# Three vector operations moved to GpSimd and two units moved to the front of an image's first attention block

## The chip, the cores and the metric

The kernel runs on one core of one Trainium2 chip. The metric is the device time of one execution in microseconds (us). Before the change it is 7322.82 us, the median of three runs (7321.42 to 7324.19).

## What is computed

Four images of 128 channels and 64 x 64 pixels go through two layers. In the first, every image is group-normalised and goes through an attention over its 4096 pixels whose keys, queries and values come from 1 x 1 convolutions. In the second, the pixels are tokens of 128 numbers. Each token is normalised, and 16 heads of 8 numbers attend over the tokens; query, key and value of a head are one and the same vector, made from cosines:

```
c = cos(heads + rx_theta);  P = cumprod(c);  z0 = prod(c[1:])
q = [z0, P[1:]]                                  # 16 heads of 8
scores = q q^T / sqrt(8);  ctx = softmax(scores) q
x1 = layernorm(x + ctx w_comb^T + b);  t = t + feed_forward(x1)
```

A recurrence over the tokens, y = sigmoid(W x + V y), ends the work. The change touches the cosine of one chunk of tokens and the order of the first work of the second layer's attention.

## The kernel before, in words

Images are worked on one after the other. For each there is a convolution stage (first_stage: the first layer, with the feed-forward of the image before woven in) and an attention stage (second_stage, which calls attention). The 4096 tokens are eight chunks of 512. For a chunk, the generator `tokens` (L465) takes the first layer's result, normalises it (statistics L249 and L250, a reciprocal root on GpSimd at L228, the normalisation L255), adds rx_theta (L518, the argument of the cosine), brings the argument into range with `cos_steps` (L233 and L234 give k, the number of turns; L235, L237 and L238 subtract k times two pi in three parts; L240 takes the magnitude), lets ScalarE take the sine (L242), multiplies the cosines up (L536 to L541), turns the result with TensorE (L273, tile pq) and writes it to DRAM as high and low parts (L557). Seven chunks are done within the convolution stage. The last one, called the tail here, is carried into the attention stage, where one step of it is taken in each turn of the attention's first block: statistics after the third unit, the normalisation and argument two turns later, then the steps of the cosine, the sine in the tenth step, the products after it.

The attention works on two heads at a time, a pair; there are eight pairs. A pair has four blocks of 1024 queries. A block is a list of units, each a pair of tiles of 128 keys, and one turn of the loop works on one unit. Since scores are symmetric, only about half of them are computed. A unit of the block's own keys (an own unit) is used once. An off unit is used twice: for its own queries, and mirrored for the queries of the other block. In a turn:

- TensorE computes the scores of a unit (L867) into two of three score tiles in PSUM, the accumulators. ScalarE exponentiates them (L879); for off units it also sums them, and some off units are split in two halves, with an instruction for each.
- TensorE weighs the values with the exponentials of the unit two turns earlier (L720).
- For an off unit, VectorE transposes its two exponential tiles (L686, in `run_flips`). Four off units make a group. Two turns after a group's fourth transposition its sixteen mirrored steps (L699, `mirror_step`) may begin; each turn does as many as a credit allows, about three. When a group's sixteen steps are done, VectorE adds the product to a running sum (L713). The transposed tiles of two groups are held at once, and so are two mirrored products. Transposes of group g wait until the steps of group g - 2 are done.

An exponential tile comes free when its weighing and its transposition are done; there are six such tiles, three units' worth, and part of the image's input tile is used as further room in some turns.

All this is written in a manual schedule: each of TensorE, ScalarE, VectorE and GpSimd works through its own queue in exactly the order in which the program states its instructions. A wait in front of one instruction holds everything behind it on that engine. In VectorE's queue, the tail's steps thus stand between the transposes.

The function `order` gives the sequence of the units in a block. In the blocks of the first half, with 16 off and 4 own units, it is four off units and an own one, four times over. `prepare` loads keys and queries for a pair, in the order in which the units ask for them. After the last pair a drain works off what is left of transposes and mirrored steps, interleaved with the next image's statistics (L307 to L321), and GpSimd gathers the sums (L747, L787, L789).

Of the kernel before, what the change touches and what calls it, by code (L numbers as in the profile page):

```python
# [13 lines left out]
ALU = mybir.AluOpType  # L14
# [8 lines left out]
ROUND = 1.5 * 2**23  # L23
# [3 lines left out]
def kernel(  # L27
# [31 lines left out]
    nc = tc.nc  # L59
# [168 lines left out]
        nc.gpsimd.tensor_tensor(r, v, minus_half[: shape[0], : shape[1]], ALU.pow)  # L228
        return r

    def cos_steps(dst, arg, k, r):

        nc.vector.tensor_scalar(k, arg, 1.0 / (2 * math.pi), ROUND, ALU.mult, ALU.add)  # L233
        nc.vector.tensor_scalar(k, k, ROUND, None, ALU.subtract)  # L234
        nc.vector.scalar_tensor_tensor(r, k, -TWO_PI_1, arg, ALU.mult, ALU.add)  # L235
        yield
        nc.vector.scalar_tensor_tensor(r, k, -TWO_PI_2, r, ALU.mult, ALU.add)  # L237
        nc.vector.scalar_tensor_tensor(r, k, -TWO_PI_3, r, ALU.mult, ALU.add)  # L238
        yield
        nc.vector.scalar_tensor_tensor(r, r, -1.0, r, ALU.mult, ALU.max)  # L240
        yield
        nc.scalar.activation(dst, r, AF.Sin, bias=half_pi[: dst.shape[0]], scale=-1.0)  # L242
# [222 lines left out]
    def tokens(im, i, sums):  # L465

        n, q, cols = im["n"], im["q"], ts(i, IC)
        last = i == NTG - 1  # L470
        yield

        pt = transposed(blocks(im["xs"][:, cols]), f"px{n}_{i}", "ps_tok")
        x0 = im["xs"][:, cols] if last else get("thalf", f"x0_{n}_{i}")
        nc.scalar.copy(x0, pt)
        yield


        total, taken = sums.pop(i), sums.pop(("sum", i))
        ps = get("ps_tok", f"sum{n}_{i}")[:, 0:P]  # L480
        tv = total.rearrange("p j (k c r) -> p j c k r", c=4, r=32)
        for j in range(2):
            for c in range(4):
                nc.tensor.matmul(
                    ps[ts(c, 32), :],
                    ones[:, 0:32],
                    tv[:, j, c],
                    start=j == 0,
                    stop=j == 1,
                    skip_group_check=True,  # L490
                )
        by_token = once.tile([P, P], F32, tag="sums", name=f"sums{n}_{i}")
        nc.vector.transpose(by_token, ps)
        if n == "r":
            inv = stats.tile([P, TG], F32, tag="inverse", name=f"inv{n}_{i}")
        else:
            inv = inverses[:, n * NIC + i, :]
        nc.vector.reciprocal(inv, by_token.rearrange("p (k r) -> p k r", k=TG)[:, :, 0])
        if not last:
            yield  # L500
        pt = transposed(blocks(taken), f"pt{n}_{i}", "ps_tok")
        if not last:
            yield
        for k in range(TG):
            at = ts(k, P)
            nc.vector.scalar_tensor_tensor(
                x0[:, at], pt[:, at], inv[:, k : k + 1], x0[:, at], ALU.mult, ALU.add
            )
        nc.sync.dma_start(out=im["x0"][:, cols], in_=x0)
        yield last  # L510
        mv, rstd = token_stats(blocks(x0), TG, 1e-5, f"t{n}_{i}")
        yield
        yield
        x1 = get("thalf", f"x1_{n}_{i}")
        normalise(blocks(x1), blocks(x0), mv, rstd, TG)
        nc.sync.dma_start(out=im["x1"][:, cols], in_=x1)
        arg, k, r = (get("thalf", f"{name}{n}_{i}") for name in ("arg", "k", "r"))
        nc.vector.tensor_tensor(  # L518
            arg.rearrange("p (a d) -> p a d", d=D),
            x1.rearrange("p (a d) -> p a d", d=D),  # L520
            rx_bc.unsqueeze(1).broadcast_to([P, IC // D, D]),
            ALU.add,
        )
        yield
        steps = cos_steps(r, arg, k, r)
        for _ in range(3):
            next(steps)
            yield

        for _ in range(3 if i == NTG - 1 else 0):  # L530
            yield
        next(steps, None)
        yield
        c = r.rearrange("p (a d) -> p a d", d=D)
        qv = q[:, cols].rearrange("p (a d) -> p a d", d=D)
        nc.gpsimd.tensor_tensor(qv[:, :, 0], c[:, :, 1], c[:, :, 2], ALU.mult)  # L536
        nc.vector.tensor_tensor(qv[:, :, 1], c[:, :, 0], c[:, :, 1], ALU.mult)
        for d in range(2, D):
            nc.vector.tensor_tensor(qv[:, :, d], qv[:, :, d - 1], c[:, :, d], ALU.mult)
            if d > 2:  # L540
                nc.gpsimd.tensor_tensor(qv[:, :, 0], qv[:, :, 0], c[:, :, d], ALU.mult)  # L541
            if d == 4:
                yield
        yield
        yield


        rows = parts_dram.rearrange("(h y d) s -> y h d s", y=2, d=D)
        pt = transposed(blocks(q[:, cols]), f"pq{n}_{i}", "ps_tok")
        high, low = get("thalf", f"high{n}_{i}"), get("thalf", f"low{n}_{i}")  # L550
        pv = pt.rearrange("p (a s c) -> p a s c", a=4, s=4)
        hv, lv = (t.rearrange("p (s a c) -> p a s c", a=4, s=4) for t in (high, low))
        nc.scalar.copy(hv.bitcast(F32R), pv)
        yield
        nc.vector.tensor_tensor(lv, pv, hv, ALU.subtract)
        for y, part in enumerate((high, low)):
            nc.sync.dma_start(out=rows[y][:, :, cols], in_=part)  # L557

    def attention(n, q, xs, tail, upcoming):
# [33 lines left out]
        def prepare(pair):  # L593

            own = qb[:, :, ts(pair, 2 * D)].rearrange("p (k a) (h d) -> p a k h d", a=4, d=D)
            qa = q_aug[pair % 2]
            qv = qa[:, 0 : NT * 2 * V].rearrange("p (k s h e) -> p s k h e", s=4, h=2, e=V)

            def copy_q(k0, k1):
                for a in range(4):  # L600
                    for s in range(4):
                        nc.gpsimd.tensor_copy(
                            qv[ts(a, 32), s, k0:k1, :, 0:D], own[ts(s, 32), a, k0:k1]
                        )

            keys = [get("keys", f"keys{n}_{pair}_{b}") for b in range(NQB)]
            queries = [get("queries", f"queries{n}_{pair}_{b}") for b in range(NQB)]
            def load_queries(b):  # L610
                for h in range(2):
                    for x in range(2):
                        for y in range(2):
                            row = ((2 * pair + h) * 2 + y) * D
                            src = parts_dram[row : row + D, ts(2 * b + x, IC)]
                            nc.sync.dma_start(
                                out=queries[b][ds(64 * h + 32 * x + 16 * y, 16), :],
                                in_=src.unsqueeze(0).broadcast_to([2, D, IC]),
                            )

            def load_keys(b):
                for h in range(2):
                    row = (2 * pair + h) * 2 * D
                    src = parts_dram[row : row + 2 * D, ts(b, QB)]
                    nc.sync.dma_start(
                        out=keys[b][ts(h, 64), :], in_=src.unsqueeze(0).broadcast_to([4, 2 * D, QB])
                    )


            there = NQB if pair else NQB - 1  # L630
            load_keys(1)
            load_queries(0)
            for b in [0] + list(range(2, there)):
                load_keys(b)
            for b in range(1, there):
                load_queries(b)
            copy_q(0, NTG if pair else NTG - 1)

            def rest():
                if pair == 0:  # L640
                    copy_q(NTG - 1, NTG)
                    load_keys(NQB - 1)
                    load_queries(NQB - 1)

            later = get("later", f"later{n}_{pair}")
            nc.gpsimd.memset(later, 0.0)
            denom = get("denom", f"denom{n}_{pair}")
            return (keys, queries, qa, later, denom), rest
# [158 lines left out]
            else:  # L807
                late.extend([mirrored, result])

        def order(b):  # L810


            own = [(QT * b + k, QT * b + TG + k) for k in range(TG)]
            halves = [(v, v) for v in range(2 * b + 2, 2 * b + (5 if b < NQB // 2 else 4))]
            halves.insert(2, (2 * b + 1, 2 * b + (5 if b < NQB // 2 else 4)))
            rest = [
                tuple(v % (2 * NQB) * TG + k for v in vs) for vs in halves for k in range(TG)
            ]
            each = len(rest) // TG
            return [u for k in range(TG) for u in rest[each * k : each * (k + 1)] + own[k : k + 1]]  # L820

# [25 lines left out]
        ready, rest = prepare(0)  # L847
        w = mirror_weights(0, 0)
        for pair in range(NPAIR):
            keys, queries, qa, later, denom = ready  # L850
            for b in range(NQB):
                block = {"acc": None}
                tiles = order(b)
                end_of_all = pair == NPAIR - 1 and b == NQB - 1

                coming = (pair, b + 1) if b < NQB - 1 else (pair + 1, 0)
# [668 lines left out]
```

## Time and profile before

| What | Value |
|---|---|
| span of the profiled run | 7316.6 us, mean granted TensorE clock 0.980 |
| TensorE busy (matmul) | 6989.7 us, 96% |
| VectorE busy | 5984.1 us, 82% |
| ScalarE busy | 5890.0 us, 81% |
| GpSimd busy | 2772.9 us, 38% |
| transposes L686 | 3584 in two groups, 1207 ns each |
| mirrored products L699 | 57344 matmuls, 1998.7 us |
| tail's argument L518 on VectorE | 4, 749 to 753 ns |

The rows of a page are averages over stages with different limits. TensorE is nearly always busy in the attention, which makes most of the time; the stretches in which it isn't are read from the timeline, where the bracket at the end of a line tells how long the engine was idle before and what it waited for. In such a line the first number is the start in us from the span's start, the second the time from start to end, and `x` counts the instructions merged in the line. In a line of the windows view stand the stretch, its length, and for each engine its busy time and its instructions, then the granted clock, the share of the DMA engines and their rate. PE is TensorE's matmuls, PEld its weight loads, DVE is VectorE, ACT is ScalarE, POOL is GpSimd.

### The profile page before, as it was taken

How to read it: one execution, taken by the hardware profiler on the slowest of the kernel's cores; microseconds unless marked ns; L12 is line 12 of the kernel's file. 1: busy time of each engine (PE TensorE's matmuls, PEld its weight loads, DVE VectorE, ACT ScalarE, POOL GpSimd, SP SyncE). 2: the span in 40 equal slices, each digit the busy share in tenths (PEclk: the TensorE clock that was granted, in tenths of full speed). 3: DMA queues.
4: the chain of work that ended last, by engine and by line, in shares of the span. 5: the costliest groups of instructions: out<-in, count | busy, mean ns of one | idle time of the engine just before them, and what ended most of it. 6: DMA issues, size and time to landing. Idle time of an engine off the chain costs nothing. (4 is left out here: it accounts for less than half of the span.)

```text
span 7316.6 us, 225003 instructions
## 1 busy us (share of the span) xinstructions
PE 6989.7 (96%) x93198; PEld 3500.9 (48%) x93198; DVE 5984.1 (82%) x8068; ACT 5890.0 (81%) x11605; POOL 2772.9 (38%) x9929
## 2 busy tenths in 40 slices
PE   8999999998999999999899999999899999999977
PEld 3445555554444555554344455555444455555546
DVE  5678899886778999888677998989777798889964
ACT  3479999994448999998444999999744599999966
POOL 1024444433223454444222354444422344444442
PEclk9999999999999999999999999999999999999988
DMA  1010000000111000000011100000001100000012
GB/s 28 32 35 24 29 20 21 21 20 14 35 40 44 27 21 20 21 24 20 18 32 48 37 21 21 20 27 18 18 26 35 44 32 21 24 29 21 11 59 105
DMA packets 81599, 212.82 MB, mean 29 GB/s; under 512 B 8800, under 2 KB 8832, under 8 KB 79792
## 3 DMA queue, kind: packets, MB, share of 16 engines
q1 hardware_dynamic: 77312, 186.68, 7.5%
q8 instruction: 733, 12.01, 0.7%
q10 hardware_dynamic: 2016, 10.49, 0.4%
q14 instruction: 306, 2.51, 0.1%
q0 software_dynamic: 1232, 1.14, 0.1%
HBM read 141.65 MB, written 56.62 MB: 27 GB/s over the span
## 5 line engine op out<-in xcount | busy, mean ns | idle before, releaser
L879 ACT ACTIVATE e<-s 128x1024 f32<-128x1024 f32 (+1 forms) x3480 | 2946.7, 889 | 59.1 <-PE s L867 35.9
L686 DVE STREAM_TRANSPOSE t<-e 128x1024 f32<-128x1024 f32 x2240 | 2586.3, 1207 | 6.3 <-ACT e L879 3.9
L699 PEld LDWEIGHTS misc<-t,mirror 128*32 128x32 f32 x57344 | 1665.3, 110 | 1403.7 <-issue 1348.6
L699 PE MATMUL misc<-t,mirror 128*32 128x128 f32 x57344 | 1998.7, 274 | 24.9 <-DVE later L713 17.4
L879 ACT ACTIVATE xs<-s 128x1024 f32<-128x1024 f32 (+1 forms) x2152 | 1834.9, 893 | 33.0 <-PE s L867 19.6
L686 DVE STREAM_TRANSPOSE t<-xs 128x1024 f32<-128x1024 f32 x1344 | 1558.2, 1207 | 2.2 <-ACT xs L879 0.8
L720 PE MATMUL acc<-e,q_aug 128*32 128x512 f32 x11360 | 1518.5, 606 | 0.0
L867 PE MATMUL s<-queries,keys 32*128 32x512 f32 x9216 | 1216.9, 494 | 4.1 <-ACT e L879 2.7
L762 POOL COPY own<-o 32x36 f32<-32x36 f32 x2048 | 429.7, 210 | 1750.3 <-DVE o L754 1670.3
L407 PE MATMUL acc<-p,asmT 128*128 128x512 f32 x2048 | 983.3, 612 | 0.0
L392 ACT ACTIVATE p<-s 128x1024 f32<-128x1024 f32 x512 | 497.1, 1022 | 558.5 <-PE s L384 549.6
L720 PE MATMUL acc<-xs,q_aug 128*32 128x512 f32 x7072 | 942.2, 605 | 0.0
L400 DVE TENSOR_TENSOR total<-total,p 128x1024 f32<-128x1024 f32 x448 | 575.2, 1284 | 295.2 <-ACT p L392 271.5
L867 PEld LDWEIGHTS s<-queries,keys 32*128 32x128 f32 x9216 | 479.8, 182 | 490.5 <-issue 367.3
L656 POOL COPY mirror<-q 32x128 f32<-32x128 f32 x2048 | 601.1, 293 | 239.0 <-PE misc L699 151.1
L787 POOL COPY other<-turned 32x64 f32<-32x64 f32 x1920 | 441.1, 230 | 629.4 <-DVE turned L777 550.3
L879 ACT ACTIVATION_READ_ACCUMULATOR e<-s 128x1 f32 x2880 | 649.9, 226 | 0.0
L407 PEld LDWEIGHTS acc<-p,asmT 128*128 128x128 f32 x2048 | 361.5, 192 | 517.2 <-issue 515.0
L384 PE MATMUL s<-e,e 64*128 64x512 f32 x2048 | 520.3, 626 | 5.6 <-DVE asmT L301 5.4
L713 DVE TENSOR_TENSOR later<-later,misc 128x128 f32<-128x128 f32 (+1 forms) x576 | 162.5, 282 | 378.1 <-PE misc L699 373.7
L747 POOL COPY by_token<-by_key 32x4 f32<-32x4 f32 x2048 | 374.5, 183 | 86.4
L720 PEld LDWEIGHTS acc<-e,q_aug 128*32 128x32 f32 x11360 | 225.7, 108 | 347.8 <-issue 330.2
(246 smaller groups left out, 4719.1 us busy)
## 6 DMA issues: line engine op xcount, KB each, us to landing
keys<-parts_dram SPq DMA_DIRECT2D x256, 256.0 KB
queries<-parts_dram SPq DMA_DIRECT2D x1024, 32.0 KB
fx<-x_dram SPq DMA_DIRECT2D x64, 256.0 KB
x_dram<-x SPq DMA_DIRECT2D x56, 256.0 KB
xs<-in_x_dram SPq DMA_DIRECT2D x16, 512.0 KB
t_dram<-t2T SPq DMA_DIRECT2D x32, 256.0 KB
t2s<-t_dram SPq DMA_DIRECT2D x16, 512.0 KB
parts_dram<-high SPq DMA_DIRECT2D x28, 256.0 KB
```

The source lines that it names most:

```text
L384: nc.tensor.matmul(s[:, j, :], e2[rows, ts(2 * jp + j, P)], e1[rows, ts(ic, IC)], start=True, stop=True,)
L392: nc.scalar.activation(p, s, AF.Exp)
L400: nc.vector.tensor_tensor(state[ic], state[ic], p, ALU.add)
L407: nc.tensor.matmul(state["acc", ic], asmT[:, ts(2 * jp + j, P)], p[:, j, :], start=jp == 0 and j == 0, stop=jp == NP - 1 and j == 1,)
L656: nc.gpsimd.tensor_copy(wv[ts(a, 32), s, :, :, ts(a, D)], own[ts(s, 32)])
L686: nc.vector.transpose(group["e"][h][:, k, :], es[h])
L699: nc.tensor.matmul(state["acc"][ts(2 * x + h, 32), :], state["w"][:, QT * (s // 4) + TG * x + s % 4, h, :], state["e"][h][:, :, ds(IC * x ...
L720: nc.tensor.matmul(it["in"]["acc"][ts(2 * h + x, 32), :], it["qa"][:, ds((2 * it["tiles"][x] + h) * V, 32)], it["e"][h][:, ts(x, IC)], sta ...
L762: nc.gpsimd.tensor_copy(own[ts(s, 32), ts(x, 4), h, :], ov[ts(2 * h + x, 32), s, :, 0:V])
L787: nc.gpsimd.tensor_copy(to[ts(k, 32), h], tv[ts(2 * x + h, 32), k])
L867: nc.tensor.matmul(ss[h][:, x, :], keys[unit[x] // QT].bitcast(F32R)[r, ts(unit[x] % QT, P)], queries[b].bitcast(F32R)[r, :], start=True, ...
L879: nc.scalar.activation(es[h][:, ts(x, IC)] if split else es[h], ss[h][:, x, :] if split else ss[h].rearrange("p x c -> p (x c)"), AF.Exp, ...
```

## The change

There are two edits. In the tail, which alone has `last` set, the argument of the cosine and the two operations that find k go to GpSimd; the other steps stay on VectorE. It is meant to relieve VectorE in the block in which the tail's steps stand among its transposes. And the first block of an image (pair 0, block 0) begins with two own units, so that work that needs no transposing comes first; then six off units, an own one, five off, an own one, five off. As own units read the block's own keys, `prepare` loads keys 0 ahead of keys 1 for the first pair, and the queries right after the first keys.

```diff
-    def cos_steps(dst, arg, k, r):
-        nc.vector.tensor_scalar(k, arg, 1.0 / (2 * math.pi), ROUND, ALU.mult, ALU.add)
-        nc.vector.tensor_scalar(k, k, ROUND, None, ALU.subtract)
+    def cos_steps(dst, arg, k, r, eng=nc.vector):
+        eng.tensor_scalar(k, arg, 1.0 / (2 * math.pi), ROUND, ALU.mult, ALU.add)
+        eng.tensor_scalar(k, k, ROUND, None, ALU.subtract)
         nc.vector.scalar_tensor_tensor(r, k, -TWO_PI_1, arg, ALU.mult, ALU.add)
...
-        nc.vector.tensor_tensor(
+        eng = nc.gpsimd if last else nc.vector
+        eng.tensor_tensor(
             arg.rearrange("p (a d) -> p a d", d=D),
...
-        steps = cos_steps(r, arg, k, r)
+        steps = cos_steps(r, arg, k, r, eng)
...
-            load_keys(1)
-            load_queries(0)
-            for b in [0] + list(range(2, there)):
+            for b in ([1, 0] if pair else [0, 1]) + list(range(2, there)):
                 load_keys(b)
+                if b == (1 if pair else 0):
+                    load_queries(0)
...
-        def order(b):
+        def order(b, very_first):
...
+            if very_first:
+                return own[:2] + rest[:6] + own[2:3] + rest[6:11] + own[3:] + rest[11:]
...
-                tiles = order(b)
+                tiles = order(b, not (pair or b))
```

## The prediction

> **What bounds the kernel now.** The windows view first (PE is TensorE): a stretch over the first block of units of the second image's attention, and one over the block behind it.
>
> ```profile
> core 0: us, PE busy (x) PEld busy (x) DVE busy (x) ACT busy (x) POOL busy (x), PEclk, DMA share, GB/s
> 2217.00:2270.00 53.00, 46.09 (x616) 21.23 (x614) 48.45 (x68) 46.53 (x94) 14.70 (x41) 0.94 0.09 29
> 2270.00:2313.00 43.00, 43.00 (x757) 22.00 (x753) 37.83 (x38) 42.10 (x89) 13.54 (x49) 1.00 0.16 58
> 2247.20:2254.02 6.82, 6.33 (x72) 3.33 (x72) 5.96 (x7) 4.39 (x11) 2.58 (x6) 0.50 0.01 2
> ```
>
> The reader is to see TensorE full in an ordinary block and not in the first, where VectorE leads and the granted clock is below 1. Taken from exponential to exponential in ScalarE's timeline, the first block lasts 50.2, 52.3, 52.4 and 52.3 us in the four images, the same block of later pairs 42.8. All that this change can touch is thus 7.4 + 3 x 9.5 = 36 us, 0.5% of the kernel. The timelines of the second image show where it goes: TensorE, VectorE (lines left out), GpSimd, ScalarE.
>
> ```profile
> 2242.10 1.06 PE L720 MATMUL acc<-e,q_aug 128*32 128x512 f32 x8
> 2247.69 1.93 PE L699 MATMUL misc<-t,mirror 128*32 128x128 f32 x32 [4.53 <-DVE later L713]
> ```
>
> ```profile
> 2221.34 6.87 DVE L686 STREAM_TRANSPOSE t<-e 128x1024 f32<-128x1024 f32 x6
> ...
> 2232.18 2.00 DVE L255 TENSOR_SCALAR room<-xs,mv_t,r_t 128x128 f32<-128x128 f32 x4
> 2234.21 0.75 DVE L518 TENSOR_TENSOR room<-room,rx_bc 128x512 f32<-128x512 f32 x1
> 2234.89 2.36 DVE L686 STREAM_TRANSPOSE t<-e 128x1024 f32<-128x1024 f32 x2
> 2237.18 0.38 DVE L233 TENSOR_SCALAR room<-room 128x512 f32<-128x512 f32 x1
> 2237.59 0.43 DVE L234 TENSOR_SCALAR room<-room 128x512 f32<-128x512 f32 x1
> ...
> 2245.10 2.36 DVE L686 STREAM_TRANSPOSE t<-xs 128x1024 f32<-128x1024 f32 x2
> 2247.38 0.25 DVE L713 TENSOR_TENSOR later<-later,misc 128x128 f32<-128x128 f32 x1
> ```
>
> ```profile
> 2231.62 1.80 POOL L590 MEMSET mirror<- 128x2048 f32 x1
> ```
>
> ```profile
> 2246.01 1.28 ACT L242 ACT_TABLE_LOAD   x1
> 2247.30 0.72 ACT L242 ACTIVATE room<-room,half_pi 128x512 f32<-128x512 f32 x1
> 2250.43 1.28 ACT L879 ACT_TABLE_LOAD   x1 [2.40 <-PE s L867]
> ```
>
> VectorE works without a pause from 2221.34 on. TensorE's second group of mirrored products needs the eighth pair of transposes, which ends at 2247.5: TensorE stands 4.53 us, and then runs at half clock for 6.82 us. A smaller term: L255 takes 2.00 us, while four STTs of its size (L506) take 1.13; the 1.80 us memset lies on it.
>
> **What the Trainium skill says.** "TensorE: Matmul & The Clock Gate", Part 1: too little activity in a window of 3.41 us halves TensorE's clock. The trace agrees: 4.53 us idle, then 0.50 for 6.82 us, two windows. "SBUF — State Buffer", Who interferes with whom: a VectorE tensor_scalar in two-port mode and a GpSimd instruction exclude each other, while a one-input instruction such as the transpose shares. It fits L255 behind the memset. "GPSIMD Engine Reference", 4.1: two-input operations are about twice as slow there, one-input ones roughly line rate. Two-input agrees: L980 takes 1.27 us on GpSimd, L518 0.75 on VectorE. "ScalarE: Activation LUTs", What ACT_TABLE_LOAD costs: 1283 ns and a drain; the trace has 1.28, twice.
>
> **The change, on the second image.** Unit costs from TensorE's starts 2233.31, 2233.75, 2234.63, 2235.40: scores 0.44, weighing 0.88, three mirror steps 0.77 (0.257 each). ScalarE: exps with sums 0.995 apart, 1.99 a unit; without 0.90, 1.8; split units 4 x 0.57.
>
> *Own units first.* Nothing to transpose in the first two turns, so the first transpose waits for ScalarE: 2217.93 + 4 x 0.90 + 0.995 + 0.12 = 2222.7, not 2221.34: **+1.4** for VectorE's queue. Mirrored work starts two turns later, so the deadline moves by two turns, worth 2 x (0.44 + 0.88) = 2.6 of TensorE's own work, and six steps (29 against 23 in turns 11/13 to 19 of the block, by the order of instructions) fall out of the block. They are not saved: that order has 23 steps after an image's last score matmul before, 29 after.
>
> *GpSimd's three operations.* VectorE loses L518 (0.68 to the next start) and L233, L234 (0.87), **-1.55**; and as GpSimd now turns to the argument, its memset no longer lies on L255, **-0.95**. Behind the three on GpSimd stand two memsets (0.59 and 1.80) and 16 mirror copies (6.4 us): from 2235.2 they end at 2244.0, ahead of the sine that the next one (L536) needs, and their weights are first used in the next block, so that shift costs nothing. The wait that comes: L235 needs k. L255 would end at 2232.4, the argument takes 1.27 (L980), k two one-input operations that this trace does not show on GpSimd. Bounds: 0.5 (half the 0.95 memset of 1024) and 1.27 (the two-input row). I take 0.65, for copies of 16 and 128 elements grow from 0.19 to 0.29. So k at 2235.2, while the pair of transposes between ends at 2234.6: **+0.6** (0.2 to 1.8).
>
> Sum: 2247.5 + 1.4 - 2.5 + 0.6 = 2247.0. VectorE gains only half a microsecond, but is asked two turns later.
>
> *TensorE's path.* Group 0 starts when the fourth pair is there, 2234.7 (2231.3 before); 16 x 0.257 + 4 x 1.32 later, 2244.1, it is done. Next is turn 13, whose second score half needs a score bank (three tiles) freed by the first exp of turn 12. On ScalarE turn 11 ends at 2243.0 (its buffer is freed by the sixth pair), then load and sine to 2245.0, load back 2246.3, half a split unit: 2247.5. **ScalarE's two table loads, hidden in TensorE's wait before, now are the wait**: 2244.3 to 2247.5, 3.2 us, most of a window, so the half clock returns. Group 1 starts at 2249.5. From there to the next block's scores: 6 x 1.32 + 23 x 0.257 + 0.58 (the q transposes) = 14.4, plus 2 for the half clock and 0.5 of short waits: 2266.4, against 2269.7. Gain **3.3** at the block's end; later blocks have the same content.
>
> *Given back.* The image ends in a drain:
>
> ```profile
> 3461.40 0.38 PE L312 MATMUL pg<-gmv,grp 128*128 128x1 f32 x2 [4.34 <-DVE gmv L310]
> ...
> 3463.55 4.75 PE L699 MATMUL misc<-t,mirror 128*32 128x128 f32 x128
> ```
>
> TensorE waits for statistics, then works off the steps left, and GpSimd's last gathers and the next image wait for them. Six more at 4.75/16 = 0.30 cost **1.8**. Net 1.5 an image. In the first image the first exponential (435.35) starts after VectorE's L506 (434.96) and not before it, as in the others, so own units first move the first transpose from 436.5 to 440.1, +3.6 instead of +1.4, and the stall on ScalarE's loads follows all the same: walked alike, its block goes from 50.2 to 48.3, and 1.9 less the drain is 0.1. Three times 1.5 and 0.1 make 5; a half clock of one window instead of two gives 1.2 more each in three images. I take 8: **7315 us**.
>
> **The rivals.** (A) as above, stall moved to ScalarE. (B) The stall splits over two windows and the clock stays full, or turn 12's exp comes sooner: 3.4 us more in each image and the drain partly hidden, 8 + 4 x 3.4 = 21, 7302. For: the windows run free of the program. Against: 3.2 us idle leave at least 1.6 in one window. (C) GpSimd's k comes late (two-input rate, 2.1 as in L997, whose row reaches 2.13 against 1.26): L235 waits up to 3 us more, the transposes behind it, the buffers of the exps and the sine all slip, and the drain is paid besides: 3.3 - 3 - 1.8 = -1.5, with a second half-clocked stretch (-3.4) about -5 an image: 7343. For: VectorE's slack in front of L235 is one pair of transposes only. Against: the transposes have one input and should not slow GpSimd. Mild forms of it end at 7320.
>
> **How the numbers follow.** A 0.60, B 0.28, C 0.12. A spans 7307 to 7321 by the bounds of k and of the half clock, all within 0.2% (14.6 us). The range, 7303 to 7322, reaches to B's value and mild C. Faster 0.30, same 0.60, slower 0.10.
>
> **What would show it.** VectorE's L713 near 2247 with no L518, L233, L234 ahead; L255 near 1.1; L235 idle before it by 0.2 to 1.8 and put down to GpSimd; TensorE's long wait put down to ScalarE in front of scores; the half clock still there; first blocks of 48 to 49.5; a drain longer by 1.5 to 2. Wrong if the first blocks fall to 45 (B), if L235's wait passes 2 us (C), or if the drain hides the six steps.

## The result, and the profile after

The changed kernel takes **7550.16 us** (median of 4 runs, 7546.17 to 7555.77), the kernel before 7323.50 beside it: ratio **1.0311, 95% interval 1.0298 to 1.0324**. It is 227 us slower. The prediction, 7315 with a range to 7322, was wrong, and by far.

The block that the prediction worked on behaves almost as it said. These are the windows of the second image, its first block and the one behind it (line numbers are one to three higher than before):

```profile
2283.00:2332.00 49.00, 42.45 (x568) 18.98 (x568) 41.55 (x62) 45.54 (x94) 18.32 (x44) 1.00 0.09 29
2332.00:2376.00 44.00, 42.96 (x756) 22.00 (x752) 38.30 (x39) 41.85 (x89) 13.52 (x49) 1.00 0.16 58
```

And these the timelines of that first block: TensorE's long wait, three steps of VectorE, two of GpSimd.

```profile
2313.97 0.50 PE L870 MATMUL s<-queries,keys 32*128 32x512 f32 x2 [3.19 <-ACT e L882]
```

```profile
2296.56 1.08 DVE L255 TENSOR_SCALAR room<-xs,mv_t,r_t 128x128 f32<-128x128 f32 x4
...
2301.37 0.69 DVE L235 SCALAR_TENSOR_TENSOR room<-room,room 128x512 f32<-128x512 f32 x1 [1.45 <-POOL room L234]
...
2312.95 0.25 DVE L714 TENSOR_TENSOR later<-later,misc 128x128 f32<-128x128 f32 x1
```

```profile
2299.14 0.62 POOL L233 TENSOR_SCALAR room<-room 128x512 f32<-128x512 f32 x1
2299.84 1.50 POOL L234 TENSOR_SCALAR room<-room 128x512 f32<-128x512 f32 x1
```

The first windows line is what was hoped for: 49 us, and a clock of 1.00. The second is the surprise. A block that the edits don't touch takes 44 us where it took 43, at nearly the same busy time (42.96 and 43.00): TensorE stands about 1 us in it. To see how much there is of this, take the time from first exponential to first exponential and add up over the four images. All from the profiled runs, in us:

| Kernel | 4 first blocks | 120 blocks between | 4 last blocks | outside | span |
|---|---|---|---|---|---|
| before | 207.2 | 4604.1 | 131.7 | 2373.6 | 7316.6 |
| after | 195.5 | 4807.0 | 164.9 | 2377.9 | 7545.3 |
| difference | -11.7 | **+202.9** | **+33.2** | +4.3 | +228.7 |

The waits view names the new wait. Its columns: the engine and line that waited, for what, us in total, times, the longest.

```profile
DVE later L714 <- PE misc L700: 736.9, 443, 5.4
...
PE acc L721 <- DVE o L755: 170.9, 124, 1.9
```

In the kernel before the same two stood the other way round, VectorE waiting for TensorE:

```profile
DVE o L754 <- PE acc L720: 127.9, 125, 1.2
```

Here o is what `finish` makes first at the end of a block: VectorE transposes the block's accumulator out of PSUM. The accumulator has one bank, so the next block's first weighing can't begin before o is done. There are 32 blocks in an image, so 31 boundaries, and 4 x 31 = 124: TensorE waits at **every** boundary. VectorE's queue at the first boundary of the second image shows why, before and after:

```profile
2311.12 2.33 DVE L686 STREAM_TRANSPOSE t<-xs 128x1024 f32<-128x1024 f32 x2
2314.79 0.58 DVE L713 TENSOR_TENSOR later<-later,misc 64x128 f32<-64x128 f32 x2 [1.33 <-PE misc L699]
2316.29 0.72 DVE L754 STREAM_TRANSPOSE o<-acc 128x512 f32<-128x512 f32 x1 [0.92 <-PE acc L720]
```

```profile
2327.28 4.61 DVE L687 STREAM_TRANSPOSE t<-e 128x1024 f32<-128x1024 f32 x4
2331.82 4.58 DVE L687 STREAM_TRANSPOSE t<-xs 128x1024 f32<-128x1024 f32 x4
2336.33 0.67 DVE L755 STREAM_TRANSPOSE o<-acc 128x512 f32<-128x512 f32 x1
2338.84 0.59 DVE L714 TENSOR_TENSOR later<-later,misc 64x128 f32<-64x128 f32 x2 [1.84 <-PE misc L700]
```

```profile
2337.05 1.07 PE L721 MATMUL acc<-e,q_aug 128*32 128x512 f32 x8 [1.04 <-DVE o L755]
```

Before, VectorE has finished the group's eight transposes at 2313.45, waits for the add, then for the accumulator: o begins as soon as there is something to transpose. After, the add has slid behind o, the eight transposes run without a gap into o, and TensorE waits for it.

The theory, then. The six mirrored steps that fall out of the first block are a **lag**. The credit of a turn (the line `rates`, 3.3 beside off units and 3.0 beside own ones) gives 16 x 3.3 + 4 x 3.0 = 64.8 for the 64 steps of a block of the first half (49.8 for 48 in the others), hardly more than is needed, and what is over is cut by a cap of 4; so the lag can stay. Counted through the program's order, what the cap cuts from the second pair on is exactly this surplus, 0.8 and 1.8 steps a block, with the lag as without. And the lag does stay: at the end of the image it is still there, for behind the last score matmul TensorE's timeline has 24 + 32 + 128 = 184 mirrored matmuls before and 24 + 80 + 128 = 232 after, at eight a step 23 and 29. A lagging group also holds back the transposes of the next but one, so all of VectorE's mirrored work is late against TensorE's own, and o with it. The rivals: GpSimd's work disturbs something; or the new order costs by itself.

### The profile page after: what moved, and what is told of

Read it like the earlier page. It is cut to its first block, busy times and chain, and to the rows that moved or that the text cites. A ratio compares the mean times of both kernels' runs of the same rounds, so it can differ in the third digit from the quotient of the medians.

```text
span 7545.3 us, 224993 instructions
## 1 busy us (share of the span) xinstructions
PE 7039.8 (93%) x93198; PEld 3525.9 (47%) x93198; DVE 5967.7 (79%) x8056; ACT 5876.9 (78%) x11605; POOL 2792.2 (37%) x9941
## 3 DMA queue, kind: packets, MB, share of 16 engines
q14 instruction: 303, 2.48, 0.1%
## 5 line engine op out<-in xcount | busy, mean ns | idle before, releaser
L870 PE MATMUL s<-queries,keys 32*128 32x512 f32 x9216 | 1238.2, 497 | 32.2 <-ACT e L882 29.1
L714 DVE TENSOR_TENSOR later<-later,misc 128x128 f32<-128x128 f32 (+1 forms) x576 | 164.9, 286 | 739.7 <-PE misc L700 736.9
L882 ACT ACTIVATION_READ_ACCUMULATOR e<-s 128x1 f32 x2880 | 669.6, 232 | 0.0
```

Source lines behind the costliest of these rows:

```text
L870: nc.tensor.matmul(ss[h][:, x, :], keys[unit[x] // QT].bitcast(F32R)[r, ts(unit[x] % QT, P)], queries[b].bitcast(F32R)[r, :], start=True, ...
L882: nc.scalar.activation(es[h][:, ts(x, IC)] if split else es[h], ss[h][:, x, :] if split else ss[h].rearrange("p x c -> p (x c)"), AF.Exp, ...
```

## The experiments

All times are medians; ratios are to the kernel before, measured beside them.

**The GpSimd edit alone.** The kernel before with the GpSimd parts of the diff only (`cos_steps` with its `eng`, and its two uses).

> The kernel before with the GpSimd edit alone: argument, k and its subtraction of the last tiles on GpSimd, loads and order of units as before. Theory (the order of the units costs the time, through a lag that is never caught up): no lag, so the boundaries between blocks look as before, with the add ahead of o on VectorE and no wait of TensorE for o; the first block of each image loses some 2 us or more of its 50.2 to 52.4 us, and the time is 7305 to 7322 us. Rival (GpSimd's work costs the time, by disturbing VectorE's memory port or by coming late): most of the 227 us is here, about 7500 us.

7318.38 us, ratio 0.9997 (0.9988 to 1.0005): no change that can be told. First blocks 200.0 in all (-7.2), the 120 between 4605.7, as before. GpSimd is not the cause.

**The order and the loads alone.**

```diff
-        eng = nc.gpsimd if last else nc.vector
+        eng = nc.vector
```

> The changed kernel with its cosine argument and range back on VectorE: only the order of units and of loads is changed. Theory (order, lag): 7545 to 7565 us, with TensorE waiting for o some 120 times, 160 to 180 us in all. Rival (GpSimd): within 20 us of the kernel before.

7560.75 us, ratio 1.0328 (1.0312 to 1.0344), and the same wait, 170.9 us in 124 times. The whole loss is in the reordering.

**The lag alone.** The kernel before, every unit where it was.

```diff
-                    pending.append((turn + 2, group["steps"], group["block"]))
+                    pending.append((turn + (2 if g else 4), group["steps"], group["block"]))
```

(`g` is counted through all of an image's blocks, so this delays one group in an image, the first, by two turns.)

> The kernel before, order of units and engines as they were, with one edit: the mirrored steps of the first group in every block fall due two turns later. Theory (the lag alone makes the loss): VectorE has o behind eight transposes at the boundaries, TensorE waits for o over 100 times, and the time is 7500 to 7560 us. Rival (what costs is in the new order or the new engine): within 30 us of the kernel before.

7563.27 us, ratio 1.0328 (1.0312 to 1.0344). The "in every block" of that text was too much: one delayed group among the 112 of an image is enough for the whole loss. From its waits:

```profile
PE acc L720 <- DVE o L754: 170.8, 124, 1.9
```

Its 120 blocks take 4800.1 us and its last ones 165.1, against 4807.0 and 164.9 in the changed kernel. The new order costs nothing beyond the lag that it makes.

**The lag taken back.** The changed kernel with more credit for two blocks of the first pair.

```diff
-                    credit = min(credit + rates[0 if off else 1], 4.0)
+                    more = 1.0 if pair == 0 and 0 < b < 3 else 0.0
+                    credit = min(credit + rates[0 if off else 1] + more, 4.0 + more)
```

> The changed kernel with more credit for the steps held back, one a turn more in blocks 1 and 2 of each image, so that the six steps that fell out of the first block are caught up there; nothing else differs. Theory (it is the lag that lasts to the end of the image): from the third block on, VectorE has the add ahead of o again, TensorE's waits for o are under 15 in all, the last block of an image takes 34 us again, and the time is 7300 to 7325 us. Rival (the order of the units costs by itself, in the first block or through what its tiles hold): stays at 7500 us or more.

7327.55 us, ratio 1.0009 (1.0001 to 1.0018), 2.5 us above what I had written. TensorE's wait for o is 2.5 us in 4 times, the last blocks take 132.0. So the loss does go with the lag; but catching up costs: the second block of an image takes 45.5 us (42.9 before) and the third 35.0 (33.8), 14.4 over the 120 blocks, more than the 10.2 won in the first ones.

**Half the lag.** The kernel of the lag alone, with 3 in place of 4.

> The kernel before with the mirrored steps of the first group of every block due one turn later, not two: half the lag (three steps); o stands behind eight transposes and ahead of the add in VectorE's queue all the same. Theory (what counts is that the two change places): nearly the whole loss, 7520 to 7565 us. Rival (the loss is in proportion to the steps held back): about 7440 us.

7323.75 us, ratio 1.0004 (0.9995 to 1.0013). **Neither theory had this.** The add stands behind o here as well, and no loss can be told. (Of the three steps two are still behind at the end of an image: 25 after the last score matmul.) VectorE's queue at a boundary, with one turn of lag and then with two:

```profile
1444.01 0.29 DVE L713 TENSOR_TENSOR later<-later,misc 128x128 f32<-128x128 f32 x1 [1.57 <-PE misc L699]
...
1451.01 2.33 DVE L686 STREAM_TRANSPOSE t<-e 128x1024 f32<-128x1024 f32 x2
1454.07 0.72 DVE L754 STREAM_TRANSPOSE o<-acc 128x512 f32<-128x512 f32 x1 [0.74 <-PE acc L720]
```

```profile
1483.37 0.29 DVE L713 TENSOR_TENSOR later<-later,misc 128x128 f32<-128x128 f32 x1 [1.58 <-PE misc L699]
...
1490.37 2.33 DVE L686 STREAM_TRANSPOSE t<-e 128x1024 f32<-128x1024 f32 x2
1492.62 0.68 DVE L754 STREAM_TRANSPOSE o<-acc 128x512 f32<-128x512 f32 x1
```

From the start of the add that opens the round to the end of the eight transposes both need the same 9.3 us. With one turn of lag they end 0.7 us before o can begin. With two turns TensorE's last weighing of the block starts at 1489.92 and takes 1.06, so the accumulator is done near 1491.0 and o is 1.6 late; TensorE has other work for a part of that and waits 1.28. It is a threshold, not a proportion: what counts is VectorE's slack ahead of o, the time between the end of the transposes and the start of o. The kernel before shows how large it is at the boundary above: the eight transposes end at 2313.45 and o starts at 2316.29, so there are **2.84 us**. A turn is 2.08 us (TensorE's scores come about that far apart). One turn of lag fits, two make 4.16 and put o 1.3 late; TensorE waited 1.04 there in the changed kernel.

The slack is not the same at every boundary. Behind the first, second, third and fourth block of a pair it is 1.92, 2.82, 3.15 and 2.48 us in the kernel before (medians from the second pair on), and TensorE's waits behind them in the changed kernel are 1.86, 1.27, 0.97 and 1.55: the smaller the slack, the longer the wait, at all four places (mean 170.9 / 124 = 1.38). One turn of lag just uses up the smallest slack: there o begins right behind the transposes, and TensorE does not wait yet.

**o ahead of two transposes, the lag kept.** At the end of a block the last two of the eight are issued after `finish`.

```diff
-                    nc.vector.transpose(group["e"][h][:, k, :], es[h])
+                    held.append((group["e"][h][:, k, :], es[h]))
+                    if at < last_at or k < TG - 1:
+                        nc.vector.transpose(*held.pop())
...
                             finish(*it["block"])
+                            while held:
+                                nc.vector.transpose(*held.pop(0))
```

> The changed kernel, lag and all, with one thing moved: at the end of each block the last two of the eight transposes ahead of o on VectorE are issued behind o. Same work. Theory (the loss is o's place in VectorE's queue): o starts up to 2.4 us sooner, TensorE's waits for o fall from 171 us to under 50, and the time falls by 100 to 180 us, to 7370 to 7450 us. Rival (the lag costs in another way and the wait for o is where it only shows): the wait moves to other lines, the time stays above 7500 us.

7343.51 us, ratio 1.0029 (1.0018 to 1.0040): 207 of the 227 us are gone, more than expected, though lag and work are the same (29 steps still follow the last score matmul of an image). No wait of TensorE's matmuls for o is listed any more, and VectorE waits for the accumulator again:

```profile
DVE o L757 <- PE acc L723: 58.8, 69, 1.3
```

The 120 blocks take 4597.7 us, 6.4 less than before the change. This is the strongest of the runs: o's place in one queue, and nothing else, carries the loss between the first block and the last.

**ScalarE empties the accumulator, the lag kept.**

```diff
+            taken = half_tile(f"acc_taken{n}_{pair}_{b}")
+            nc.scalar.copy(taken, block["acc"])
             o = half_tile(f"o{n}_{pair}_{b}")
-            nc.vector.transpose(o, block["acc"])
+            nc.vector.transpose(o, taken)
```

> The changed kernel, lag and all, where ScalarE first copies a block's accumulator to SBUF and VectorE transposes the copy, so that TensorE's next block waits for ScalarE's copy and not for VectorE's queue (one buffer of queries fewer makes the room). Theory (the wait of TensorE for o is the loss): of the 171 us of waits and the 25 us of half clock with them most goes, a copy of 0.5 to 1 us a block comes in on ScalarE: 7370 to 7450 us. Rival: ScalarE's queue is as deep at the boundary as VectorE's, the wait only changes its name: above 7500 us.

7410.04 us, ratio 1.0118 (1.0103 to 1.0134), as the theory said. The wait is shorter and has another name:

```profile
PE acc L721 <- ACT acc_taken L755: 66.8, 124, 0.7
```

The 120 blocks take 4671.9 us, 67.8 more than before: the wait, and hardly anything beside it.

**The lag caught up within the first block.** The changed kernel with the fourth own unit at the end of the first block and one step a turn more of credit in that block.

```diff
-                return own[:2] + rest[:6] + own[2:3] + rest[6:11] + own[3:] + rest[11:]
+                return own[:2] + rest[:6] + own[2:3] + rest[6:] + own[3:]
...
+                    more = 1.0 if not (pair or b) else 0.0
```

> The changed kernel with the fourth own unit of the first block at its end, as in the other blocks, and one step a turn more of credit in that block alone, so that the steps held back are done before it ends; add ahead of o at every boundary from the first on. Theory: TensorE makes the six steps in the first block (1.5 us of the 3.6 gained there), all later blocks are as in the kernel before, the first blocks last 49.5 to 51.5 us and the time is 7310 to 7320 us. Rival (filling the first block brings its stalls back, or the extra credit delays scores there): 7320 to 7335 us.

7322.82 us, ratio 1.0001 (0.9993 to 1.0010): between the two, with the rival's reason. All later blocks are as before (4605.6 and 131.8), but the first take 51.5 to 52.0, and almost the whole gain is gone. TensorE does the steps sooner, so it reaches the scores that stand behind ScalarE's two table loads sooner, and waits longer there:

```profile
2252.30 0.79 PE L870 MATMUL s<-queries,keys 32*128 32x512 f32 x2 [3.84 <-ACT e L882]
```

```profile
2250.97:2257.80 6.83, 5.50 (x58) 2.80 (x62) 6.73 (x11) 4.74 (x16) 1.59 (x4) 0.50 0.01 2
```

A wait of 3.84 us comes with 6.83 us of half clock; the wait of 3.19 us in the changed kernel came with none (1.00 over its whole first block). But the half clock is the smaller part of the 2.8 us by which these blocks are longer than the changed kernel's 48.8. The kernel of the lag taken back has the changed kernel's first block, with the same wait; in the second image 6.83 us of half clock come with it and in the third none, and these blocks take 49.84 and 48.74 us. That is 1.1 us. The six steps themselves are 1.5 (at 0.257 each), and the wait is 0.65 longer: together a little more than the 2.8. So part of what the changed kernel wins in its first block is only put off with the steps.

**What is left: the last block of an image.** The kernel of o_ahead, with the lag taken back in the third block of the last pair.

```diff
-                last_at = 99 if pair == NPAIR - 1 and b == NQB - 1 else len(tiles) - 2
+                last_at = 99 if pair == NPAIR - 1 and b in (2, 3) else len(tiles) - 2
...
+                    more = 1.0 if pair == NPAIR - 1 and b in (2,) else 0.0
```

> The kernel of o_ahead (o issued ahead of two transposes, lag kept) with the lag taken back before the last block of each image: one step a turn more of credit in the third block of the last pair, and o back in its old place from there on. Theory (what is left of the loss, 22 us, is the last block of each image, 5.6 to 8.3 us longer, where the exponentials have only the e buffers and the held-back transposes keep them): the last block takes 34 us again, the third block of the last pair 1.5 to 2.7 us more, and the time is 7305 to 7322 us. Rival (the last block is longer for another reason than the lag): it stays above 39 us, and the time above 7335 us.

**7309.09 us, ratio 0.9983 (0.9977 to 0.9990)**: better than both kernels, by 0.17% than the one before. The last blocks take 130.3 us in all where they took 161.2, the third block of the last pair 36.05 (33.85 in the other pairs), the first ones 197.9. In the changed kernel the last block holds this wait, which is gone with the lag:

```profile
3556.83 0.50 PE L870 MATMUL s<-queries,keys 32*128 32x512 f32 x2 [2.77 <-ACT e L882]
```

There the exponentials have only the six e tiles, and ScalarE waited in turn 3.06 us for a transposition to free one. TensorE's waits in that block, this one and three shorter ones, come to 4.3 of the 8.2 us by which it is longer in the second image; 3.41 us at half clock are part of the rest, and what remains was not taken apart.

**An aside on GpSimd.** L234 takes 1.50 us there, L233 0.62, on tiles of the same size; on VectorE, in the other chunks, the medians are 427 and 421 ns.

```diff
-        eng.tensor_scalar(k, k, ROUND, None, ALU.subtract)
+        eng.tensor_scalar(k, k, ROUND, 0.0, ALU.subtract, ALU.add)
```

> The kernel of ahead_caught with the subtraction of k given a second operation, an addition of 0. On GpSimd the first tensor_scalar, with two operations, takes 0.62 us, the subtraction with one alone 1.50 us, on tiles of the same size, while on VectorE the two differ by under 0.05 us. Theory (the form with one operation is the slow one there): the subtraction takes about 0.6 us, and VectorE's wait in front of L235 falls from 1.4 us to 0.6 or less. Rival (it is slow because it works in place, or stands behind something): it stays near 1.5 us. The time of the whole moves by a few us at most.

One run: 7308.63 us. The subtraction took 1.93 us and VectorE's waits in front of L235 grew from 5.8 to 7.5 us. The theory of the short form fell. Why L234 is slow stays open; that it works in place, as L233 does not, was not tried.

## Why the prediction was wrong, point by point

- **The step that failed** is half a sentence: "later blocks have the same content". The content is the same, but its place against TensorE's own work is not. The six steps were counted, 29 against 23, both counts are in the timelines, and they were booked where the lag ends, in the drain, and not in the 31 boundaries and the last block that it travels through. Its two terms, +202.9 and +33.2 us, are not in the sum at all, and no rival looked outside the first block and the drain. Hence the 36 us, "all that this change can touch", were a bound on the gain, taken for a bound on the change.
- What the 202.9 us consist of: 166.9 of the 170.9 us of waits for o lie in these 120 blocks (the rest in the last ones). The clock makes up what is left: in these blocks the clock records have no stretch at half clock before, and 22 of 3.41 us after, which cost half of their 75 us, 37.5. Together 204, about the whole. With a wait for o of the same length, 1.9 us, some second blocks of a pair take 44.8 us and others 46.3 or 46.4. Windows of one of each, with the granted clock, and then of 3.41 us around the wait of each and behind it:

```profile
2650.75:2697.16 46.41, 44.55 (x756) 22.66 (x757) 39.50 (x44) 42.07 (x88) 21.34 (x84) 0.96 0.03 8
2811.64:2856.43 44.79, 42.92 (x756) 21.97 (x756) 39.49 (x44) 42.06 (x88) 21.25 (x84) 1.00 0.03 8
2653.70:2657.11 3.41, 1.55 (x44) 1.03 (x40) 3.19 (x4) 3.23 (x8) 2.83 (x13) 1.00 0.12 36
2657.11:2660.52 3.41, 3.41 (x36) 1.57 (x28) 0.39 (x2) 0.13 (x2) 2.96 (x13) 0.50 0.00 0
2814.12:2817.53 3.41, 1.85 (x44) 1.04 (x36) 3.41 (x4) 3.22 (x7) 2.80 (x15) 1.00 0.09 35
2817.53:2820.95 3.42, 3.11 (x52) 1.48 (x56) 1.53 (x4) 1.51 (x3) 2.99 (x12) 1.00 0.03 8
```

In this trace every stretch at half clock begins on one grid of 3.413 us (within 0.012), the prediction's window. The first wait, 2655.1 to 2656.9, lies whole between two points of the grid, and the clock is halved behind it; the second, 2816.0 to 2817.8, lies across a point. So it goes with all 28 waits of 1.85 to 1.89 us behind the first block of a pair: the 22 that lie whole between two points are followed by 3.41 us at half clock, the 6 that lie across one, with at most 1.70 us on a side, are not. In the two slower relatives the same holds for 55 of 56.

- The drain: 1.8 expected. From L312 to the end of the mirrored products it takes 8.48 us after (3581.67 to 3590.15) and 6.90 before (3461.40 to 3468.30), **+1.6**. Right.
- VectorE's queue in the first block: L255 at 1.08 us, right. L235's wait was taken as 0.6 (0.2 to 1.8) and measured 1.45: inside the bounds, but L234 on GpSimd was taken as 0.65 and is 1.50. L714 comes 29.8 us after the block's first exponential; 29.1 were expected (2247.0 less 2217.93), and the difference, 0.7, is about that term.
- TensorE's stall moves to ScalarE's table loads, 3.2 us expected, 3.19 measured. Right; the sine and the next exponential start 1.29 and 1.30 us after their loads do, so nothing is added to a load's 1.28 us. That the half clock follows this stall was wrong, in all four images: it lies across a point of the grid each time, with 1.60 to 1.71 us on the longer side. The prediction's sum, at least 1.6 us in one window, was right, and 1.6 us was too little. This is what rival B had said of the clock, and it is luck where the grid lies: in the kernel with order and loads alone the same wait has 1.74 to 2.24 us on the longer side, and 3.41 us at half clock follow in every image. The first blocks at 48.8 us (49.3 in the first image) lie where they were expected all the same, not at B's 45, because two other things cost what the clock didn't: the stall ends 30.8 us after the block's first exponential and not 29.6, and at full clock TensorE is then early for the tail's products and waits for VectorE before it turns them:

```profile
2322.09 0.63 PE L273 MATMUL pq<-ident,q 128*128 128x128 f32 x4 [1.56 <-DVE q L540]
```

- The chances: rival C, the one on the slower side, expected VectorE to wait for GpSimd. It does, by 1.45 us, and the GpSimd edit alone costs nothing that can be measured. That rival had the side right for a reason that had no part in the result. (The range was said to reach to B's value, 7302; it begins at 7303. Nothing hangs on it.)
- What could have been read blind: the 2.84 us between the end of the eight transposes and o in the kernel before. The prediction itself had mirrored work starting "two turns later". Two turns of 2.08 against 2.84 of slack gives 1.3 us at each of 124 boundaries, 164 us, from lines that were at hand. That this lies so near to the 170.9 is in part luck: 2.84 is the slack of one boundary, and TensorE waits somewhat less than o is late.

One thing stays open: outside the attention blocks the kernels differ by up to 22 us (the kernel with the lag alone has 2393.6 there, the one with order and loads alone 2392.3, the changed one 2377.9, the best one 2371.4). It explains the 10 us between the changed kernel and its two slower relatives. It goes with the clock: outside these blocks TensorE is at half clock for 254 us in the changed kernel, 264 before and 274 in the best one, but for 308 (order and loads alone), 322 (lag alone) and 311 in the kernel with o ahead, which has 2391.0 us there. Why it falls so was not traced.

## What to carry to other kernels

A schedule that meters work by a rate hardly above its demand, and cuts what is over, can have no restoring force, as here: a delay put in once stays until the end, and must be priced at every place that it passes, not only where it comes out. So when an edit shifts one stream of work against another, list the buffers that they hand each other (here one accumulator bank) and read from the trace of before the slack ahead of each hand-over, which can differ from place to place; compare it with the shift, because up to the slack the shift is free and beyond it most of the excess is paid every time round. And if such a wait is found, moving the one instruction that frees the buffer ahead of work that isn't urgent can be worth more than removing the delay: two transposes changed places with o and 207 us came back.

## What was not expected of the hardware

A tensor_scalar with one operation took 2.4 times as long on GpSimd as one with two (1.50 and 0.62 us, 128x512), while VectorE takes 0.43 and 0.42; a second operation added to the slow one made it 1.93. And a wait of one length can be cheap or dear: the 3.19 us in the first block left the clock at 1.00 in the changed kernel and brought 3.41 or 6.83 us at 0.50 in others, and a wait of 1.9 us for o did either from block to block, by whether it lay whole between two points of a grid of 3.413 us.
